# Distances in four row groups and messages by Strassen's product between the gates' products, in the last phase of a two-layer graph network

## The chip, the cores and the metric

The kernel runs on one core of a Trainium2 chip. The metric is the device time of one execution in microseconds (us), and less is better. A core has five engines, each with its own queue that it works through in order: PE (TensorE, matrix products; its weight loads are listed as PEld), DVE (VectorE), ACT (ScalarE), POOL (GpSimd) and SP (which here issues DMAs). They wait for each other by semaphores. PE writes only to PSUM, which has eight banks of 512 float32 values on each of 128 partitions; DVE and ACT read PSUM, POOL doesn't.

## The reference

There are 128 graphs of 128 nodes with 256 features, all in float32. Layer 0 mixes a graph product with a dense one under a gate, then a layer norm. Layer 1 is the part that matters here (the batch dimension is left out):

```python
s = x @ w_se.T + b_se                                   # 3 coordinates per node
sq = sum(s * s)
dist = sq[:, None] + sq[None, :] - 2.0 * s @ s.T
A = exp(-dist) * mask                                   # mask is the adjacency
msg = relu(x @ w_msg.T + b_msg)                         # 256 -> 256
x_nmp = A @ msg
x_conv = relu(bn(conv1d(relu(bn(conv1d(x, w1))), w2, 17 taps)) + x)
gi = concat(x_conv, x_nmp) @ w_ih.T + b_ih              # 512 -> 768
gh = x @ w_hh.T + b_hh                                  # 256 -> 768
r, z = sigmoid(gi_r + gh_r), sigmoid(gi_z + gh_z)
n = tanh(gi_n + r * gh_n)
x = layernorm(x + (1 - z) * n + z * x)
```

## The kernel before

Three phases follow one another. The first (to some 745 us) computes layer 0 and the first convolution, two graphs at a time, and stores x, its transpose and, in `H`, spectral coefficients. The second (L503 to L530) does the 17-tap convolution as products of coefficients. The third, from L601 on, is the one that is changed. It works on groups of G = 4 graphs, 32 groups (`g`), and the order of PE's work in it is written out by hand (`manual_schedule`, L830 to L859); the order on the other engines is left to the scheduler.

For a group g the loop does, on PE: `l1_gather(g)` (L748), which multiplies messages by the kernel matrix `AT`, 8 products of 128 columns; the messages of the next group, `l1_project(g+1)` (L693), 8 products of 256 columns into two banks; the first half of the gates, `l1_gru(g, 0)` (L775); the distances of the next group, `l1_kernel(g+1)` (L735), one product of 512 columns over all 128 rows; after every odd group the convolution's way back for two groups, `l1_synth` (L662); and the second half of the gates, `l1_gru(g, 1)`.

The gates use Strassen's product already: a 2x2 block product is made from seven products of sums of blocks. `l1_sums` (L762) makes four sums of each left factor (kind "h" of x1T and "c" of the convolution on POOL, "m" of the gathered messages on DVE), `l1_factors` (L617) those of the weights. `product(i)` (L781) then accumulates three products of 384 columns in one bank, and DVE combines the seven banks: L797 to L801, L804 and L805, with two sums on POOL (L802, L803). The order of issue is 0, 1, 5, 6, 4, 3, 2. After that come the gates' functions, the "tail" of a half group: ACT L808, DVE L815 and L816, ACT L817, DVE L819 to L822, the norm's statistics on DVE (L247, L248), a power on POOL (L152, L153), DVE L255, ACT L257 and the store (L825).

PSUM in this phase is two pools of four banks. `psC` (`bankc`, L611) serves everything but the convolution: each product takes a bank that is given back when its last reader is done, and PE has to wait for that. `acc` (L608) holds the four banks of `l1_synth`, which DVE reads at L686.

For the distances, `left` and `right` (L542 on) hold eight values per node and graph. `l1_own` (L715) transposes 16 graphs at a time (128 rows: 16 graphs x 8 values), and POOL makes `own` (L729): 128 x 512, where for each of the four graphs all rows but its own eight are masked to zero. So one product over 128 rows gives four graphs' distances, and ACT takes the exponential (L743), DVE multiplies by the adjacency (L744).

Of the kernel before, what the change touches and what calls it, by code (L numbers as in the profile page):

```python
# [14 lines left out]
P = 128  # L15
D = 256
NC = D // P
J = 2
# [2 lines left out]
CO = 3  # L21
KD = 8
GD = P // KD
PAD = TAPS // 2
L = P + PAD
M = L
# [7 lines left out]
def gnn_layers_kernel(ctx: ExitStack, tc: tile.TileContext, a: dict, out: bass.AP):  # L34
# [332 lines left out]
    def l1_front(p):  # L367
        s = st[p]
        h = s["h"] = wk.tile([P, J, D], F32, tag="h", name=f"h_{p}")
        for j in range(J):  # L370
            ph = bank(f"conv1_ps_{p}_{j}")
            for c in range(NC):
                nc.tensor.matmul(  # L373
                    ph[:, 0 : D + CO], lhsT=s["x1T"][:, c, nodes(j)], rhs=conv1_w[:, c, :],
                    start=(c == 0), stop=(c == NC - 1),
                )
            nc.vector.tensor_tensor(h[:, j, :], ph[:, 0:D], shift1, ALU.add)
            nc.scalar.activation(coords[:, p * J + j, :], ph[:, D : D + CO], AF.Copy)
        nc.scalar.activation(h, h, AF.Relu)

    def l1_store(p):
# [173 lines left out]
    nc.vector.tensor_add(left[:, :, CO + 1], left[:, :, CO + 1], coords[:, :, 2])  # L555
    nc.vector.tensor_copy(right[:, :, CO], left[:, :, CO + 1])

    mask_i = cw.tile([P, GD], I32, tag="mask_i", name="mask_i")
    nc.gpsimd.iota(mask_i, pattern=[[-KD, GD]], base=0, channel_multiplier=1)
    mask_f = cw.tile([P, GD], F32, tag="mask_f", name="mask_f")  # L560
    nc.vector.tensor_copy(mask_f, mask_i)
    mask = cw.tile([P, GD], F32, tag="mask", name="mask")
    nc.vector.tensor_scalar(mask, mask_f, 0.0, None, ALU.is_ge)
    nc.vector.scalar_tensor_tensor(mask, mask_f, float(KD - 1), mask, ALU.is_le, ALU.mult)
    w_msg = weights("w_msgT", D)
    b_msg = rows("L1_gnn_b_msg", 0, D, cw)


    def gate_weights(name, lo_n, lo_rz):
# [35 lines left out]
    ci = cpool("ci", 3)  # L605
    cy = cpool("cy", 4)
    ck = cpool("ck", 2)
    acc = cpool("acc", 4, space=PSUM)  # L608
    psc = cpool("psC", 4, space=PSUM)

    def bankc(name):  # L611
# [2 lines left out]
    cs = cpool("cs", 1)  # L614
    factors = {}

    def l1_factors():  # L617

        for kind, w in (("h", w_hh), ("c", w_ih[:, 0:NC]), ("m", w_ih[:, NC : 2 * NC])):
            t = cs.tile([P, 4, 3 * P], F32, tag=f"t{kind}", name=f"t_{kind}")  # L620
            b11, b12, b21, b22 = (w[:, c, h, :] for c in range(NC) for h in range(2))
            nc.vector.tensor_sub(t[:, 0, :], b12, b11)
            nc.vector.tensor_sub(t[:, 1, :], b22, t[:, 0, :])
            nc.vector.tensor_sub(t[:, 2, :], b22, b12)
            nc.vector.tensor_sub(t[:, 3, :], t[:, 1, :], b21)
            factors[kind] = (b11, b21, b22, t[:, 3, :], t[:, 0, :], t[:, 1, :], t[:, 2, :])

    def load_c(g):
        s = st[g] = {}
# [30 lines left out]


    def l1_synth(d):  # L662
        pcs = {}
        for e in range(2):
            s = st[2 * d + e]
            for c in range(NC):
                pc = pcs[e, c] = acc.tile([P, 512], F32, tag="acc", name=f"conv2_ps_{2 * d + e}_{c}")
                for q in range(G):
                    nc.tensor.matmul(  # L669
                        pc[:, nodes(q)], lhsT=sy[2 * d + e][0][:, q, c * P : (c + 1) * P], rhs=S,  # L670
                        start=(q == 0), stop=False, skip_group_check=True,
                    )
        for q in range(G):
            for e in range(2):
                for c in range(NC):
                    k = slice(32 * (NC * e + c), 32 * (NC * e + c) + ML)
                    nc.tensor.matmul(
                        pcs[e, c][:, nodes(q)], lhsT=sy[2 * d + e][1][k, q, :], rhs=SL[k, :],
                        start=False, stop=(q == G - 1), skip_group_check=True,
                    )  # L680
        for e in range(2):
            s = st[2 * d + e]
            s["xcT"] = ck.tile([P, NC, G * P], F32, tag="xcT", bufs=3, name=f"xcT_{2 * d + e}")
            for c in range(NC):
                dst = s["xcT"][:, c, :]
                nc.vector.scalar_tensor_tensor(  # L686
                    dst, pcs[e, c], scale2[:, c : c + 1], s["x1T"][:, c, :], ALU.mult, ALU.add
                )
                nc.scalar.activation(dst, dst, AF.Relu, bias=shift2[:, c : c + 1])
            l1_sums(2 * d + e, "c", s["xcT"], nc.gpsimd)  # L690


    def l1_project(g):  # L693
        s = st[g]
        x1T = s["x1T"]
        l1_sums(g, "h", x1T, nc.gpsimd)
        msg = ck.tile([P, G, D], F32, tag="msg", name=f"msg_{g}")
        for pr in range(G // 2):
            pm = bankc(f"msg_ps_{g}_{pr}")
            for j in range(2):  # L700
                q = 2 * pr + j
                for c in range(NC):
                    nc.tensor.matmul(  # L703
                        pm[:, j * D : (j + 1) * D], lhsT=x1T[:, c, nodes(q)], rhs=w_msg[:, c, :],
                        start=(c == 0), stop=(c == NC - 1),
                    )
            nc.vector.tensor_tensor(
                msg[:, 2 * pr : 2 * pr + 2, :], pm.rearrange("p (j e) -> p j e", j=2),
                b_msg.unsqueeze(1).to_broadcast([P, 2, D]), ALU.add,
            )  # L710
        nc.scalar.activation(msg, msg, AF.Relu)
        s["msg"] = msg


    def l1_own(g):  # L715
        if g % (GD // G) == 0:
            pt = bankc(f"turn_ps_{g}")
            for i, v in enumerate((left, right)):
                nc.tensor.transpose(
                    pt[:, nodes(i)], v[:, g * G : g * G + GD, :].rearrange("p q k -> p (q k)"), ident  # L720
                )
            turned = ck.tile([P, 2, P], F32, tag="turned", name=f"turned_{g}")
            nc.scalar.activation(turned.rearrange("p i n -> p (i n)"), pt[:, 0 : 2 * P], AF.Copy)
            st["turned"] = turned
        turned = st["turned"]

        own = ck.tile([P, G, P], F32, tag="own", name=f"own_{g}")
        lo = g * G % GD
        nc.gpsimd.tensor_tensor(  # L729
            own, turned[:, 1, :].unsqueeze(1).to_broadcast([P, G, P]),  # L730
            mask[:, lo : lo + G].unsqueeze(2).to_broadcast([P, G, P]), ALU.mult,
        )
        st[g].update(turned=turned, own=own)

    def l1_kernel(g):  # L735
        s = st[g]
        turned, own = s["turned"], s["own"]
        pd = bankc(f"dist_ps_{g}")
        nc.tensor.matmul(  # L739
            pd, lhsT=turned[:, 0, :], rhs=own.rearrange("p q n -> p (q n)"), start=True, stop=True  # L740
        )
        AT = ck.tile([P, G * P], F32, tag="AT", name=f"AT_{g}")
        nc.scalar.activation(AT, pd, AF.Exp, scale=-1.0)  # L743
        nc.vector.tensor_mul(AT, AT, s["adjT"].rearrange("p q n -> p (q n)"))  # L744
        s["AT"] = AT

# [15 lines left out]
    def l1_sums(g, kind, src, engine):  # L762

        v = src.rearrange("p c (r j n) -> p c r j n", r=G // 2, j=2)
        a11, a12, a21, a22 = (v[:, c, :, j, :] for j in range(2) for c in range(NC))
        t = ck.tile([P, 4, G // 2, P], F32, tag=f"s{kind}", name=f"s{kind}_{g}")
        s1, s2, s3, s4 = (t[:, i] for i in range(4))
        engine.tensor_tensor(s1, a21, a22, ALU.add)
        engine.tensor_tensor(s2, s1, a11, ALU.subtract)
# [2 lines left out]
        st[g][f"f{kind}"] = (a11, a12, s4, a22, s1, s2, s3)  # L772


    def l1_gru(g, pr):  # L775
        s = st[g]
        x1 = s["x1"]
        y = ck.tile([P, 2, D], F32, tag="y", name=f"y_{g}_{pr}")
        add, sub = ALU.add, ALU.subtract

        def product(i):  # L781
            pg = bankc(f"g_ps_{g}_{pr}_{i}")
            for k, (kind, lo) in enumerate((("h", 0), ("c", P), ("m", P))):
                nc.tensor.matmul(  # L784
                    pg[:, lo : lo + 3 * P], lhsT=s[f"f{kind}"][i][:, pr, :], rhs=factors[kind][i],
                    start=(k == 0), stop=(k == 2), skip_group_check=True,
                )
            return pg
# [38 lines left out]
            del st[g]  # L827

    ND = NG // 2
    with tc.manual_schedule(engines={mybir.EngineType.PE}):  # L830
        load_c(0)
        load_c(1)
        load_y(0)
        for g in range(2):
            load_x1(g)
            l1_own(g)
        for g in range(2):
            l1_project(g)
        for g in range(2):
            l1_kernel(g)  # L840
        l1_factors()
        l1_synth(0)
        for g in range(NG):
            d = g // 2
            if g + 2 < NG:
                load_c(g + 2)
                if g % 2 == 0:
                    load_y(d + 1)
                load_x1(g + 2)
            l1_gather(g)  # L850
            if 2 <= g + 1 < NG:
                l1_own(g + 1)
                l1_project(g + 1)
            l1_gru(g, 0)
            if 2 <= g + 1 < NG:
                l1_kernel(g + 1)
            if g % 2 == 1 and d + 1 < ND:
                l1_synth(d + 1)
            l1_gru(g, 1)  # L859
# [42 lines left out]
```

## Time and profile before

| what | us |
|---|---|
| runs (3): lowest, median, highest | 2086.69, 2088.59, 2091.08 |
| profiled execution, its time | 2086.79 |
| profiled execution, its span | 2085.0 |
| mean granted TensorE clock | 0.994 of full |
| last phase, from the first message product to the end | 929.5 to 2085.0 |
| PE busy from 1000 to 2000 us | 1000.0 |
| DVE busy from 1000 to 2000 us | 700.5 |
| POOL busy from 1000 to 2000 us | 402.4 |
| ACT busy from 1000 to 2000 us | 266.1 |

The span goes from the first to the last instruction of the profiled execution; 1.8 us of its time lie outside. An engine's busy time is what its instructions took; a bracket behind a line of a timeline tells how long the engine sat idle before it and what ended the wait. A matmul of the program in float32 stands as two passes in the trace. Matmuls overlap, so their costs are read from the start of one to the start of the next.

### The profile page before, as it was taken

How to read it: one execution, taken by the hardware profiler on the slowest of the kernel's cores; microseconds unless marked ns; L12 is line 12 of the kernel's file. 1: busy time of each engine (PE TensorE's matmuls, PEld its weight loads, DVE VectorE, ACT ScalarE, POOL GpSimd, SP SyncE). 2: the span in 40 equal slices, each digit the busy share in tenths (PEclk: the TensorE clock that was granted, in tenths of full speed). 3: DMA queues.
4: the chain of work that ended last, by engine and by line, in shares of the span. 5: the costliest groups of instructions: out<-in, count | busy, mean ns of one | idle time of the engine just before them, and what ended most of it. 6: DMA issues, size and time to landing. Idle time of an engine off the chain costs nothing.

```text
span 2085.0 us, 27437 instructions
## 1 busy us (share of the span) xinstructions
PE 2043.7 (98%) x9025; PEld 1401.6 (67%) x9025; DVE 1433.0 (69%) x2856; ACT 744.0 (36%) x1484; POOL 672.9 (32%) x889
## 2 busy tenths in 40 slices
PE   8999999999999979999999999999999999999997
PEld 5666666766667658886666666666666666666664
DVE  7777777776777744447776766676767767766766
ACT  3555555555555511112222222222222222222221
POOL 1111111111111135553343444343434434443432
PEclk9999999999999999999999999999999999999999
DMA  3444444344444469993222122212212221221100
GB/s 117 137 145 138 137 147 144 133 144 137 140 145 133 153 228 318 305 302 119 62 82 68 54 74 72 69 60 72 78 51 75 70 73 56 67 72 56 36 25 21
DMA packets 191789, 235.39 MB, mean 113 GB/s; under 512 B 16400, under 2 KB 136736, under 8 KB 191648
## 3 DMA queue, kind: packets, MB, share of 16 engines
q1 hardware_dynamic: 186160, 229.44, 33.5%
q10 hardware_dynamic: 5488, 4.21, 0.7%
q8 instruction: 72, 1.18, 0.2%
q14 instruction: 69, 0.57, 0.1%
HBM read 129.77 MB, written 103.81 MB: 112 GB/s over the span
## 4 chain that ended last, share of the span: by engine, by line
PE 95%; DVE 2%; DMA 2%; ACT 1%; issue 1%; POOL 0%; POOLq 0%; ACTq 0%; DVEq 0%; SPq 0%
PE g_ps L784 42%; PE f_ps L303 10%; PE msg_ps L703 5%; PE gate_ps L308 5%; PE conv_ps L373 5%; PE y_ps L510 5%; PE mix_ps L329 3%; PE coef_ps L391 3%; PE nmp_ps L754 3%; PE conv_ps L669 3%; PE z_ps L523 2%; PE w_ps L408 2%; PE x1T_ps L270 2%; PE wl_ps L411 1%; PE xT_ps L270 1%; PE dist_ps L739 1%
## 5 line engine op out<-in xcount | busy, mean ns | idle before, releaser
L303 PE MATMUL f_ps<-w,xT 128*128 128x512 f32 x512 | 244.1, 600 | 0.1
L808 ACT ACTIVATE o<-o 128x1024 f32<-128x1024 f32 x64 | 67.6, 1057 | 335.6 <-DVE o L805 335.6
L152 POOL TENSOR_SCALAR rstd_b<-mv_b 128x2 f32<-128x2 f32 x64 | 12.2, 191 | 501.6 <-DVE mv_b L248 501.6
L152 POOL TENSOR_SCALAR rstd_a<-mv_a 128x2 f32<-128x2 f32 x64 | 12.2, 191 | 463.9 <-DVE mv_a L248 447.9
L784 PE MATMUL g_ps<-t_c,sc 128*128 128x384 f32 x384 | 155.2, 486 | 0.0
L784 PE MATMUL g_ps<-t_m,sm 128*128 128x384 f32 x384 | 155.2, 486 | 0.0
L784 PE MATMUL g_ps<-t_h,sh 128*128 128x384 f32 x384 | 155.2, 486 | 0.0
L257 ACT ACTIVATE y<-y,nb_b,rstd_b 128x256 f32<-128x256 f32 x128 | 69.9, 593 | 218.6 <-DVE nb_b L255 218.6
L308 PEld LDWEIGHTS gate_ps<-w,xT 128*128 128x128 f32 x512 | 98.2, 192 | 69.2 <-issue 61.8
L510 PE MATMUL y_ps<-wb,H 128*128 128x256 f32 x544 | 128.9, 380 | 4.7 <-DMA wb<-w_d 2.1
L308 PE MATMUL gate_ps<-w,xT 128*128 128x256 f32 x512 | 132.2, 381 | 0.0
L802 POOL TENSOR_TENSOR u<-u,p 128x512 f32<-128x512 f32 x64 | 81.1, 1267 | 155.4 <-DVE p L801 155.4
L303 PEld LDWEIGHTS f_ps<-w,xT 128*128 128x128 f32 x512 | 88.6, 192 | 62.6 <-issue 62.2
L312 ACT ACTIVATE hom<-f_ps,norm 128x256 f32<-128x256 f32 x128 | 60.5, 473 | 187.0 <-PE f_ps L303 187.0
L518 POOL TENSOR_TENSOR ws<-wb 128x512 f32<-128x512 f32 x67 | 94.8, 1416 | 88.7 <-PE z_ps L523 60.3
L373 PE MATMUL conv_ps<-conv_w,x1T 128*128 128x259 f32 x512 | 122.6, 381 | 0.0
L510 PEld LDWEIGHTS y_ps<-wb,H 128*128 128x128 f32 x544 | 102.8, 190 | 20.5 <-issue 5.1
L703 PE MATMUL msg_ps<-w_msgT_w,cx1T 128*128 128x256 f32 x512 | 115.6, 379 | 0.0
L784 PEld LDWEIGHTS g_ps<-t_m,sm 128*128 128x128 f32 x384 | 73.0, 190 | 50.9
L784 PEld LDWEIGHTS g_ps<-t_c,sc 128*128 128x128 f32 x384 | 73.0, 190 | 50.9
L784 PEld LDWEIGHTS g_ps<-t_h,sh 128*128 128x128 f32 x384 | 72.9, 190 | 50.9 <-issue 1.2
L373 PEld LDWEIGHTS conv_ps<-conv_w,x1T 128*128 128x128 f32 x512 | 97.2, 190 | 14.4
(219 smaller groups left out, 4622.4 us busy)
## 6 DMA issues: line engine op xcount, KB each, us to landing
wb<-w_d SPq DMA_DIRECT2D x68, 512.0 KB
w_d<-w_o SPq DMA_DIRECT2D x256, 128.0 KB
y_d<-yb SPq DMA_DIRECT2D x68, 256.0 KB
x<-in_x SPq DMA_DIRECT2D x64, 256.0 KB
x_d<-x SPq DMA_DIRECT2D x64, 256.0 KB
x1T_d<-x1T SPq DMA_DIRECT2D x64, 256.0 KB
cx1T<-x1T_d SPq DMA_DIRECT2D x64, 256.0 KB
yt<-y_d SPq DMA_DIRECT2D x32, 512.0 KB
```

The costliest lines, as they stand in the source:

```text
L257: nc.scalar.activation(dst[:, q, :], src[:, q, :], AF.Identity, bias=nb[:, q : q + 1], scale=rstd[:, q : q + 1],)
L270: nc.tensor.transpose(t[:, (c * J + j) * P : (c * J + j + 1) * P], src[:, j, c * P : (c + 1) * P], ident,)
L303: nc.tensor.matmul(pf, lhsT=xT[:, c, nodes(j)], rhs=w0[:, c, 0 : 2 * D], start=(c == 0), stop=(c == NC - 1),)
L308: nc.tensor.matmul(pg[:, j * D : (j + 1) * D], lhsT=xT[:, c, nodes(j)], rhs=w0[:, c, 2 * D : 3 * D], start=(c == 0), stop=(c == NC - 1),)
L329: nc.tensor.matmul(pm[:, j * D : (j + 1) * D], lhsT=adjT_[:, j, :], rhs=hom[:, j, :], start=True, stop=True,)
L373: nc.tensor.matmul(ph[:, 0 : D + CO], lhsT=s["x1T"][:, c, nodes(j)], rhs=conv1_w[:, c, :], start=(c == 0), stop=(c == NC - 1),)
L510: nc.tensor.matmul(py[:, blk, :], lhsT=coefs(blk if k == 0 else 2 * k + 1 - blk, c), rhs=w[:, c, blk, :], start=(c == 0), stop=(c == NC - 1),)
L518: nc.gpsimd.tensor_tensor(ws, w[:, :, 0, :], w[:, :, 1, :], ALU.add)
L703: nc.tensor.matmul(pm[:, j * D : (j + 1) * D], lhsT=x1T[:, c, nodes(q)], rhs=w_msg[:, c, :], start=(c == 0), stop=(c == NC - 1),)
L784: nc.tensor.matmul(pg[:, lo : lo + 3 * P], lhsT=s[f"f{kind}"][i][:, pr, :], rhs=factors[kind][i], start=(k == 0), stop=(k == 2), skip_grou ...
L802: nc.gpsimd.tensor_tensor(u4, u2, p5, add)
L808: nc.scalar.activation(rz, rz, AF.Tanh, scale=0.5)
```

## The change

Distances: the 16 transposed graphs are put in another order (`coords` gets a slot that is worked out from the graph's number), so that the four graphs of a group lie in four different groups of 32 rows. `own` becomes 128 x 128, made by one masked multiplication on POOL, and the product becomes four of 32 rows and 128 columns, each into a bank of its own; they use the four banks of `acc`, now one tile, in turn with the synthesis. `l1_own` is called two groups ahead, and the distances come right after the gather.

Messages: seven products of sums (of 128 columns, for each of two pairs of graphs) in place of eight blocks, from the same sums of x1T that the gates use, which are now made two groups ahead and kept in three buffers. DVE combines seven pieces of 128 x 256, with two sums on POOL. The products are made in four portions, each with a bank of `psC`: 0 and 1, 5 and 6, 4 and 3, and 2. A portion is issued ahead of each of the first four gate products of `l1_gru(g, 0)`. The sums of kind "m" get one buffer in place of two.

```diff
+            b = p * J + j
+            slot = b // GD * GD + b % G * GR + b % GD // G
+            nc.scalar.activation(coords[:, slot, :], ph[:, D : D + CO], AF.Copy)
...
-    acc = cpool("acc", 4, space=PSUM)
+    acc = cpool("acc", 1, space=PSUM)
...
+        def products(*which):
+            pm = bankc(f"msg_ps_{g}_{which[0]}")
+            for k, i in enumerate(which):
+                for r in range(2):
+                    nc.tensor.matmul(
+                        pm[:, (2 * k + r) * P : (2 * k + r + 1) * P],
+                        lhsT=s["fh"][i][:, r, :], rhs=m_factors[i], start=True, stop=True,
+                    )
...
+        pa, pb = products(0, 1)
+        v.tensor_tensor(u1, pa, bias_m[:, 0].to_broadcast([P, 2, P]), add)
+        v.tensor_tensor(o[:, :, 0, 0, :], pb, u1, add)
+        yield
+        pa, pb = products(5, 6)
+        v.tensor_tensor(u2, pa, u1, add)
+        v.tensor_tensor(u3, pb, u2, add)
+        yield
+        pa, pb = products(4, 3)
+        v.tensor_tensor(p5, pa, bias_m[:, 1].to_broadcast([P, 2, P]), add)
+        v.tensor_tensor(o[:, :, 1, 0, :], u3, pb, sub)
+        nc.gpsimd.tensor_tensor(u4, u2, p5, add)
+        nc.gpsimd.tensor_tensor(o[:, :, 1, 1, :], u3, p5, add)
+        yield
+        (pa,) = products(2)
+        v.tensor_tensor(o[:, :, 0, 1, :], pa, u4, add)
         nc.scalar.activation(msg, msg, AF.Relu)
...
+        own = ck.tile([P, P], F32, tag="own", name=f"own_{g}")
+        nc.gpsimd.tensor_scalar(
+            own, turned[:, 1, :], mask[:, g % GR : g % GR + 1], None, ALU.mult
+        )
...
+        pd = acc.tile([P, G, 512], F32, tag="acc", name=f"dist_ps_{g}")
+        for q in range(G):
+            k = slice(q * P // G, (q + 1) * P // G)
+            nc.tensor.matmul(
+                pd[:, q, 0:P], lhsT=turned[k, 0, :], rhs=own[k, :], start=True, stop=True
+            )
...
-    def l1_gru(g, pr):
+    def l1_gru(g, pr, between=()):
...
         def product(i):
+            next(between, None)
...
+                l1_own(g + 2)
+                l1_sums(g + 2, "h", st[g + 2]["x1T"], nc.gpsimd)
             l1_gather(g)
             if 2 <= g + 1 < NG:
-                l1_own(g + 1)
-                l1_project(g + 1)
-            l1_gru(g, 0)
-            if 2 <= g + 1 < NG:
                 l1_kernel(g + 1)
+            l1_gru(g, 0, l1_project(g + 1) if 2 <= g + 1 < NG else ())
```

At the start of the phase, where there are no gates yet, the first two groups' portions are issued one after another, each group followed by its distances.

## Prediction

> **What bounds the kernel now.** First the busy shares of the page, then the same by stretch of the last phase: the stretch table's columns are the stretch, its length, and busy time (instructions) of PE, weight loads, DVE, ACT and POOL, then TensorE's granted clock, DMA share and GB/s.
>
> ```profile
> PE 2043.7 (98%) x9025; PEld 1401.6 (67%) x9025; DVE 1433.0 (69%) x2856; ACT 744.0 (36%) x1484; POOL 672.9 (32%) x889
> ```
>
> ```profile
> 1500.00:2000.00 500.00, 500.00 (x2109) 329.77 (x2108) 349.50 (x631) 133.13 (x201) 200.17 (x239) 1.00 0.19 61
> ```
>
> PE has no idle at all over 500 us of the phase that is changed, at full clock, so a shorter product list shortens the kernel as long as PE stays fed. But DVE stands at 70% (349.5 of 500): it reads every product out of PSUM and does the gates' arithmetic, and an engine at 70% on average is at 100% somewhere. So next comes the timeline, by engine, for one even-numbered group (start, length, then the work; x16 counts passes, a product in the program being two passes):
>
> ```profile
> 1509.99 1.95 PE L754 MATMUL nmp_ps<-AT,msg 128*128 128x128 f32 x16
> 1511.77 3.62 PE L703 MATMUL msg_ps<-w_msgT_w,cx1T 128*128 128x256 f32 x16
> 1515.23 0.81 PE L784 MATMUL g_ps<-w_hhT_w,cx1T 128*128 128x384 f32 x2
> ...
> 1528.78 1.02 PE L739 MATMUL dist_ps<-own,turned 128*128 128x512 f32 x2
> 1529.63 0.81 PE L784 MATMUL g_ps<-w_hhT_w,cx1T 128*128 128x384 f32 x2
> ```
>
> Lengths overlap, so prices are start to start: gather 16 passes of 128 columns 1.78 (0.111 a pass), messages 3.46, distances 0.85; seven gate products take 13.55 (1515.23 to 1528.78), 1.935 each. Call T the end of the gather (here 1511.77). DVE from T on:
>
> ```profile
> 1512.15 0.71 DVE L815 SCALAR_TENSOR_TENSOR o<-o 128x512 f32<-128x512 f32 x1 [1.20 <-ACT o L808]
> 1512.79 0.95 DVE L770 TENSOR_TENSOR sm<-nmpT 128x256 f32<-128x256 f32 x1
> 1513.66 1.21 DVE L816 SCALAR_TENSOR_TENSOR o<-o 128x512 f32<-128x512 f32 x1
> 1514.80 0.95 DVE L768 TENSOR_TENSOR sm<-nmpT 128x256 f32<-128x256 f32 x1
> 1515.67 0.68 DVE L707 TENSOR_TENSOR msg<-msg_ps,L_gnn_b_msg_b 128x512 f32<-128x512 f32 x1
> ...
> 1518.74 0.68 DVE L707 TENSOR_TENSOR msg<-msg_ps,L_gnn_b_msg_b 128x512 f32<-128x512 f32 x1
> 1519.34 0.67 DVE L822 TENSOR_TENSOR y<-o,cx 128x512 f32<-128x512 f32 x1
> 1519.94 0.68 DVE L797 TENSOR_TENSOR u<-g_ps,bias 128x512 f32<-128x512 f32 x1
> 1520.54 0.73 DVE L247 BATCH_NORM_STATS2 stats_b<-y 128x6 f32<-128x256 f32 x2
> 1521.20 0.16 DVE L248 BATCH_NORM_AGGREGATE mv_b<-stats_b 128x2 f32<-128x6 f32 x1
> 1521.28 0.65 DVE L798 TENSOR_TENSOR o<-g_ps,u 128x512 f32<-128x512 f32 x1
> ```
>
> The reader is to see that there is no idle bracket after the first line: from T+0.38 DVE works without a gap through the gates' tail of the previous half group (L815 to L822), and reads the first gate product (L797) only at T+8.17, 2.8 us after PE finished it. Today that is harmless: messages come first, and PE asks for that bank again only for its fifth gate product, at T+3.46+4x1.935 = T+11.2.
>
> **The change, part by part.** PE's list first. *Messages*: 8 products of 256 columns (3.46) become 14 of 128 columns, 28 passes x 0.111 = 3.11: 0.35 less. *Distances*: one product of 512 columns (0.85) becomes four of 32 rows. The trace has two such row-group stages:
>
> ```profile
> 706.63 1.14 PE L408 MATMUL w_ps<-wt,T 17*128 17x512 f32 x8
> 707.71 1.04 PE L411 MATMUL wl_ps<-wt,TL 128*32 128x512 f32 x2
> ```
>
> Eight passes of 512 columns took 1.08 where one after another at 0.425 would take 3.40, and two rounds of four 0.85; so rounds run four at a time, with 0.23 on top. (L677, 32 passes of 128 columns, gives the same: 1.10 = 8 x 0.107 + 0.24.) Four products are 8 passes: 2 x 0.107 + 0.23 = 0.45, so 0.40 less; bounds 0.28 (a quarter of L677) and 0.89 (no overlap at all, 0.04 more than now). The Trainium skill, TensorEngine Tiling (Array Packing), Key Properties, speaks against small tiled stages: a change of tiling mode drains TensorE. The 0.23 agrees with such a drain; without the rule's drain the stage would be 0.21 and the kernel, were PE the bound, some 7 us shorter by that page.
>
> If PE stayed fed, a group would lose 0.75. It will not. The gate products (G1 to G7) now have the message portions M1 to M4 between them: distances, M1, G1, M2, G2, M3, G3, M4, G4 to G7; all go through the same four banks of PSUM. In the built program M3 takes M1's bank, G3 takes G1's, M4 takes G2's, G4 M2's. A portion fills a bank in 0.89 us where a gate product fills it in 1.935, so the ring comes round sooner. PE, unhindered, wants M1's bank at T+0.45+0.89+1.935+0.89+1.935 = T+6.1 and G1's at T+7.0 (0.89 later); today it wants G1's at T+11.2.
>
> And DVE, in the order it now has: the same tail, then M1's first read, L822, M1's second read, both L247, one L248, then G1's read (L797). The first L707 of the listing is replaced by the distances' multiplication (L744, also 128x512). From rows: M1's first read starts where the second L707 stood, T+6.97; start to start 0.33 for 128x256 (L769 to L820 in the trace) and 0.60 for 128x512: L822 at 7.30, M1's second read 7.90 to 8.31, L247 twice 8.23 to 8.89, L248 to 8.97, G1's read 8.97 to 9.65. So M3 starts at 8.36, not 6.1, and G3 at 9.7, not 7.0. Then the second L248 and M2's first read, and L255, which must wait for POOL's two small operations: L255 starts 1.10 after L248 ends in the trace (its idle bracket), here at 10.84. Behind it in DVE's queue stands G2's read, 10.91 to 11.59, and M2's second, to 11.92. G3 ends at 11.63, M4 11.65 to 12.1, G4 to G7 4 x 1.935 = 7.74, to 19.85; two restarts at about 0.1 (the first pass after the 0.20 idle at 946.41 lasted 0.10 longer) make 20.0. Before, the half group with messages and distances ended at 3.46+13.55+0.85 = T+17.85. **An even group costs 2.15 more**, though PE has 0.75 less to do.
>
> Odd groups: the tail there is less slowed by POOL. Over 26 groups of the trace G1's read starts at T+8.17 in even groups, T+7.05 in odd ones, and T+8.65 in every second odd one, where POOL makes two 128x512 masks (L729, 1.04 each and more); these masks shrink to 128x128, so I take 7.05 for all odd groups: everything is 1.12 earlier, the group costs 2.15-1.12 = 1.03, say 1.05, more. 15 even and 15 odd groups carry messages between gates (groups 1 to 30): 15 x 2.15 + 15 x 1.05 = **+48**.
>
> The second half group has no portions; G1's bank is asked for 7.74 after its product starts, as now. With the synthesis (L669, L677) before it DVE is done 0.5 before PE asks (1503.65 against 1504.18): the distances no longer stand ahead of it (PE 0.85 sooner), nor L744 (DVE 0.6 sooner). Margin about 0.2: nothing added, at most 0.5 x 15 = 8.
>
> Edits with one answer: coordinates' slots, sums of x1T a group earlier (POOL at 40%, inputs landed a group ahead), one set of gathered sums instead of two (PE has read the old set before the gather ends), distances in the synthesis' four banks (13 us apart): nothing, hidden under PE. DVE gets 7 reads of 128x256 (0.41) for 2 of 128x512 (0.68), +1.5 a group, counted above where it stands ahead of a bank. POOL gets two sums of 0.73 and loses about as much on the masks.
>
> *Start of the phase*: no gates yet, so portions wait for DVE and POOL openly. POOL makes 12 sums (0.73 each, from 928.0) before the first mask, so first distances at 937.4; the second group's four portions (3.1), its distances, and the exponential that frees the banks put the synthesis at about 942.6, against 938.1: +4.5 (0 if POOL's order cost nothing, 8 if a load is late).
>
> Sum: span 2085.0 + 48 + 4.5 = 2137.5. The profiled execution took 2086.79, 1.8 over its span, and the median of the runs, 2088.59, another 1.8: 2137.5 + 3.6 = **2141**. The bounds of DVE's tail: at the unslowed lengths (0.42 for the L770 and L768 sums, 0.69 for L816) it ends 1.2 sooner, 36 us over 30 groups, but odd groups have little left to win: 15 x 1.2 + 15 x 0.5 = 26 less, 2115. With every odd group as at T+8.65, 15 x 1.6 = 24 more, 2165.
>
> **Rivals.** *DVE keeps up* (faster): it decides if M1 is read by T+6.1 and G1 by T+7.0. Then 30 x 0.75 = 22 less and 4.5 more at the start: 2071. For it: PE's list is surely shorter. Against: even the best row (7.05 + 0.8 + 0.68) frees G1 at 8.5. *The clock falls*: PE would idle 2.3 us in even groups, 1.1 in odd. The trace has an idle of 1.79 (at 774.15) after which four passes took 1.10 against 1.03, and one of 3.38 (at 17.25) after which PE lost some 1.8 in the next 4 us. 2.3 is nearer to the first, so I take nothing; else 15 x 1.8 = 27 more, 2168, and at most 30 x 1.8 = 54, 2195. The Trainium skill, TensorE: Matmul & The Clock Gate, Why this matters for your kernels, wants no idle above some 3 us; by that page also nothing is added. *Row groups do not overlap*: in groups that wait for DVE the distances lie before the wait, so 0.45 or 0.89 gives the same 2141; only if DVE kept up would it cost 30 x 0.44 = 13, 2084.
>
> **How the numbers follow.** Forecast 0.70 (own range 2115 to 2165); clock 0.12; DVE keeps up 0.10, with overlap or without; a wait so small that gain and loss cancel 0.03; a still shorter tail, 2095 to 2115, 0.05. Range 2105 to 2195. Some 0.2% is what a measurement of this kernel tells from no change: faster 0.10, within 0.03, slower 0.87.
>
> **What would show it.** In the changed profile PE's busy share in the last phase falls below 95%, with idle ended by DVE ahead of the third portion (released by its second message read) and of the third gate product (by L797's successor), near 2.3 and 0.4 us in even groups, less in odd; a group pair takes some 3.2 us longer. Distances start to start near 0.45, a portion 0.89. Wrong if PE shows no idle between portions, or if first reads of G1 start before T+7.

## The result, and the profile after

The changed kernel takes **2161.46 us** (median of 4 runs, 2159.23 to 2165.97) against 2088.74 us for the kernel before (4 runs, 2086.69 to 2091.08): a ratio of 1.0351, with a 95% interval of 1.033 to 1.0372. The span of the profiled execution is 2161.0 us, where it was 2085.0, and the mean granted TensorE clock 0.986, where it was 0.994.

The page of the changed kernel first: busy shares, and the shares of the chain of work that ended last.

```profile
PE 2060.4 (95%) x9601; PEld 1414.4 (65%) x9601; DVE 1476.9 (68%) x3024; ACT 745.0 (34%) x1484; POOL 722.4 (33%) x953
...
PE 68%; DVE 17%; POOL 5%; issue 3%; ACT 3%; DMA 3%; SPq 0%; ACTq 0%; POOLq 0%; DVEq 0%
```

The same stretch of the last phase as before, in the stretch table:

```profile
1500.00:2000.00 500.00, 474.95 (x2233) 313.92 (x2233) 345.92 (x661) 124.25 (x187) 205.48 (x246) 0.99 0.20 62
```

And the waits of PE from 940 to 2100 us (who waited for whom: us in total, times, longest):

```profile
PE msg_ps L717 <- DVE msg L730: 54.7, 30, 2.8
```

PE, which had no idle here, now idles 25 of 500 us, and the chain runs through DVE for 17% of the span. All of the named wait has one place, ahead of a message portion (L717), and one releaser, DVE's second read of a portion (L730). It comes once in each of the 30 groups that carry portions. The timeline of PE for an even-numbered group shows which portion:

```profile
1550.84 1.95 PE L790 MATMUL nmp_ps<-AT,msg 128*128 128x128 f32 x16
1552.72 0.50 PE L773 MATMUL dist_ps<-own,turned 32*128 32x128 f32 x8
1553.15 1.16 PE L717 MATMUL msg_ps<-w_msgT_w,cx1T 128*128 128x128 f32 x8
1554.15 0.81 PE L823 MATMUL g_ps<-w_hhT_w,cx1T 128*128 128x384 f32 x2
...
1556.09 1.05 PE L717 MATMUL msg_ps<-t_msg,sh 128*128 128x128 f32 x8
1556.98 0.81 PE L823 MATMUL g_ps<-w_hhT_w,cx1T 128*128 128x384 f32 x2
...
1558.27 0.81 PE L823 MATMUL g_ps<-w_ihT_w,nmpT 128*128 128x384 f32 x2
1561.87 1.20 PE L717 MATMUL msg_ps<-t_msg,sh 128*128 128x128 f32 x4 [2.79 <-DVE msg L730]
1562.86 1.06 PE L717 MATMUL msg_ps<-t_msg,cx1T 128*128 128x128 f32 x4
1563.71 1.48 PE L823 MATMUL g_ps<-t_h,sh 128*128 128x384 f32 x2
1564.99 0.85 PE L823 MATMUL g_ps<-t_c,sc 128*128 128x384 f32 x2
```

With T = 1552.72, the first and second portion and two gate products go through, and the third portion stands 2.79 us. Read on behind the idle: its two halves take 0.99 and 0.85 from start to start, 1.84 together, where the second portion took 0.89 for as much, and the first third of the gate product after them 1.28 where it takes 0.645. For some 3 us the products run at half speed. The stretch table shows why: the granted clock of this stretch is 0.50.

```profile
1561.65:1565.06 3.41, 3.19 (x11) 2.61 (x12) 2.60 (x10) 0.57 (x2) 0.92 (x2) 0.50 0.41 154
```

So the wait has a second price. This group has the longest idle of all; 13 of the even groups from 2 to 28 have 2.50 to 2.65, group 30 has 0.66. DVE in the same group:

```profile
1553.36 1.06 DVE L854 SCALAR_TENSOR_TENSOR o<-o 128x512 f32<-128x512 f32 x1 [1.20 <-ACT o L847]
...
1557.21 0.68 DVE L780 TENSOR_TENSOR AT<-AT,cadjT 128x512 f32<-128x512 f32 x1
...
1560.38 0.41 DVE L729 TENSOR_TENSOR mu<-msg_ps,L_gnn_b_msg_b 128x256 f32<-128x256 f32 x1
1560.72 0.67 DVE L861 TENSOR_TENSOR y<-o,cx 128x512 f32<-128x512 f32 x1
1561.32 0.41 DVE L730 TENSOR_TENSOR msg<-msg_ps,mu 128x256 f32<-128x256 f32 x1
...
1562.39 0.65 DVE L836 TENSOR_TENSOR u<-g_ps,bias 128x512 f32<-128x512 f32 x1
```

From the first line to the first gate product's read (L836) DVE has no idle. It works off the tail of the previous half group and the distances' multiplication (L780), and comes to the first portion, whose last pass on PE ends at 1554.31, only at 1560.38.

Where the 76.0 us of the span came from, measured from gather to gather:

| part | before | after | times | sum |
|---|---|---|---|---|
| even groups with portions, mean | 33.19 | 36.66 | 15 | +52.1 |
| odd groups with portions (with the synthesis), mean | 38.16 | 39.44 | 15 | +19.1 |
| first gather of the phase | 942.87 | 948.11 | 1 | +5.2 |
| group 0, whose gates carry no portions | 29.45 | 28.98 | 1 | -0.5 |

### The profile page after: what moved, and what is told of

Read it like the earlier page. It is cut to its first block, busy times and chain, and to the rows that moved or that the text cites. A ratio compares the mean times of both kernels' runs of the same rounds, so it can differ in the third digit from the quotient of the medians.

```text
span 2161.0 us, 28880 instructions
## 1 busy us (share of the span) xinstructions
PE 2060.4 (95%) x9601; PEld 1414.4 (65%) x9601; DVE 1476.9 (68%) x3024; ACT 745.0 (34%) x1484; POOL 722.4 (33%) x953
## 3 DMA queue, kind: packets, MB, share of 16 engines
q8 instruction: 77, 1.26, 0.2%
## 4 chain that ended last, share of the span: by engine, by line
PE 68%; DVE 17%; POOL 5%; issue 3%; ACT 3%; DMA 3%; SPq 0%; ACTq 0%; POOLq 0%; DVEq 0%
PE g_ps L823 27%; PE f_ps L304 10%; PE y_ps L513 5%; PE conv_ps L374 5%; PE gate_ps L309 5%; PE mix_ps L330 3%; PE coef_ps L394 3%; PE z_ps L526 2%; ACT o L847 2%; DVE o L855 2%; PE w_ps L411 2%; DVE o L854 2%; PE x1T_ps L271 2%; PE wl_ps L414 1%; DVE o L860 1%
## 5 line engine op out<-in xcount | busy, mean ns | idle before, releaser
L823 PE MATMUL g_ps<-t_h,sh 128*128 128x384 f32 x384 | 162.9, 507 | 2.4
L717 PE MATMUL msg_ps<-t_msg,sh 128*128 128x128 f32 x384 | 58.9, 293 | 57.4 <-DVE msg L730 54.7
L717 PEld LDWEIGHTS msg_ps<-t_msg,sh 128*128 128x128 f32 x384 | 53.1, 202 | 83.1 <-issue 71.0
```

What stands on the lines that cost most here:

```text
L717: nc.tensor.matmul(pm[:, (2 * k + r) * P : (2 * k + r + 1) * P], lhsT=s["fh"][i][:, r, :], rhs=m_factors[i], start=True, stop=True,)
L823: nc.tensor.matmul(pg[:, lo : lo + 3 * P], lhsT=s[f"f{kind}"][i][:, pr, :], rhs=factors[kind][i], start=(k == 0), stop=(k == 2), skip_grou ...
```

## The experiments

The theory: PE stands because portions and gate products share a ring of four PSUM banks that DVE empties behind the previous half group's tail, and most of the longer of these idles lower PE's clock. The rivals: DVE's load of seven message reads in place of two is itself too much; the new products are dear on PE by themselves; the distances' move is the loss. Each run's ratio is to the kernel before, run beside it on the same chip.

**1. One product later, same ring (shift1).** The portions stand ahead of the second to fifth gate product:

```diff
+    def later(n, portions):
+        for _ in range(n):
+            yield
+        yield from portions
...
-            l1_gru(g, 0, l1_project(g + 1) if 2 <= g + 1 < NG else ())
+            l1_gru(g, 0, later(1, l1_project(g + 1)) if 2 <= g + 1 < NG else ())
```

> Control for the run with banks of their own: the portions stand ahead of the second to fifth gate product as there, but still in the common ring of four banks. If it is the ring that counts, TensorE still waits in every group (the third portion and the product after it stand behind the bank of the first portion and of the second gate product, which VectorE empties behind the same tail): between 2120 and 2170 us. If it was only the order (one product later), it falls to about 2070 us like the run with banks of their own.

Measured: 2124.13 us (2 runs), ratio 1.0175 (1.0153 to 1.0198). The waits of PE in the last phase:

```profile
PE g_ps L823 <- DVE u L836: 32.7, 29, 2.0
```

The wait is still in nearly every group, now ahead of the third gate product and for the first gate product's reader (L836). So a shift alone gives back half of the loss, and the ring remains.

**2. Three products later, same ring (late).** As above with `later(3, ...)`: the portions stand ahead of the fourth to seventh gate product.

> The changed kernel with its portions ahead of the fourth to seventh gate product, in the common ring. By the theory TensorE asks for the first gate product's bank at about 7.2 us after the gather, and VectorE, with no message read in front of that read, frees it at about 8 us in even groups and 7 us in odd ones: a wait of under 1 us in even groups, hardly any in odd ones, so 2070 to 2100 us, far below the changed kernel. By the rivals (VectorE's load, or dear products) it stays near 2160 us.

Measured: 2090.14 us, ratio 1.0012 (1.0002 to 1.0022). DVE's reads and PE's products are as many as in the changed kernel, and all but 3 of its 73 us are gone. The waits of PE in the last phase:

```profile
PE g_ps L823 <- DVE u L836: 5.4, 14, 0.4
PE g_ps L823 <- DVE sm L805: 1.6, 7, 0.2
```

Even groups (33.6 and 33.75) wait a little and are 0.5 us longer than before; odd ones (37.5 and 37.72) don't wait and are 0.56 shorter. That a group without a wait is shorter speaks against dear products; that the time falls this far with the same reads, against DVE's load.

**3. Banks of their own (banks, then banks2).** From the third group on the portions go to the four `acc` banks, which hold the distances and the synthesis and are idle in between; one product later, as in run 1, which is the control for it. In the first form the four banks were one tile:

```diff
+            if g < 2:
+                pm = bankc(f"msg_ps_{g}_{which[0]}")
+            else:
+                if not own_banks:
+                    four = acc.tile([P, 4, 512], F32, tag="acc", name=f"msg_ps_{g}")
+                    own_banks.extend(four[:, n, :] for n in range(4))
+                pm = own_banks.pop(0)
```

> The changed kernel with one thing different: from the third group on the four message portions are written into the four PSUM banks that the distances and the synthesis use (idle while a half group's gates run), and stand ahead of the second to fifth gate product instead of the first to fourth. TensorE's products and VectorE's reads are the same in number and size. Theory (TensorE waits because portions and gate products share a ring of four banks that VectorE empties late): the idle ahead of the portions is gone, TensorE is near 99% busy in the last phase, and the kernel falls below the one before: 30 groups x 0.75 us less, 5 us more at the start of the phase, near 2070 us. Rival (VectorE's load of seven reads instead of two is itself too much): the wait only moves to another product, the time stays above 2130. Rival (the new products are dear on TensorE by themselves, by their row groups or their small size): also unchanged, near 2160, with TensorE busy and not idle.

Measured: 2246.89 us, ratio 1.0764 (1.0748 to 1.078), far from what any theory gave. The waits of PE:

```profile
PE msg_ps L725 <- DVE msg L738: 118.2, 30, 4.9
```

This is the *second* portion waiting for the reads of the *first*, although they lie in different banks: in the program the second portion's first product waits on VectorE's semaphore for the read of the first. The two are parts of one tile, and with four tiles, below, that wait is gone. The run prices a longer wait, and says nothing on the ring. The second form has four separate tiles:

```diff
-    acc = cpool("acc", 1, space=PSUM)
+    acc = cpool("acc", 4, space=PSUM)
...
+                pm = acc.tile([P, 512], F32, tag="acc", name=f"msg_ps_{g}_{which[0]}")
...
+        pd = [acc.tile([P, 512], F32, tag="acc", name=f"dist_ps_{g}_{q}") for q in range(G)]
...
+        for q in range(G):
+            nc.scalar.activation(AT[:, nodes(q)], pd[q][:, 0:P], AF.Exp, scale=-1.0)
```

> As the first run with banks of their own, but the four banks are four separate tiles (the distances too, with four exponentials of 128x128 instead of one of 128x512), since as parts of one tile the program made the second portion wait until VectorE had read the first. Theory: TensorE is fed, and only its own list counts: in the trace of the run with portions before the fourth to seventh gate product, groups without a wait are 0.57 us shorter than before (the distances bring 0.2 instead of 0.4), so 30 x 0.57 = 17 us less and 5 more at the start of the phase: near 2076 us. Rival (VectorE's seven reads are too much wherever the banks are): TensorE idles again ahead of a gate product, 2100 us or more.

Measured: 2075.33 us (5 runs, 2071.82 to 2077.1), ratio 0.994 (0.9927 to 0.9953). In the stretch table PE is busy without gap at full clock, and DVE busier than in either kernel (369.72 of 500):

```profile
1500.00:2000.00 500.00, 500.00 (x2408) 336.42 (x2407) 369.72 (x709) 139.55 (x249) 228.30 (x271) 1.00 0.20 61
```

With the ring parted and nothing taken from DVE or PE, the loss turns into a gain. Against run 1, which differs only in the banks and in the four tiles and four exponentials that go with them, it is 49 us. That shows the ring as the cause, and DVE's load falls as a rival. A pair of groups takes 70.14 to 70.35 us where it took 71.25 to 71.47, so 0.56 less a group.

**4. PE kept busy through the wait (fill).** In even groups from the third on, the second portion's products are issued four times with the same values: useless work of 2.67 us.

```diff
+            again = 4 if which[0] == 5 and g % 2 and g > 1 else 1
+            for k, i in [(k, i) for _ in range(again) for k, i in enumerate(which)]:
```

> The changed kernel, but in every even-numbered group from the third on the products of the second portion are issued four times (same values, 24 more passes of 128 columns, 2.67 us of work that adds nothing), so that TensorE is busy while the third portion's bank is still being read. If the time is set by the bank's release and TensorE's clock falls after the idle of 2.5 to 2.8 us (some 1.5 us lost in 10 of 15 even groups), the work is free and the fall goes: 10 to 15 us less than the changed kernel, near 2148 us. If the clock had no part in it, the time is the changed kernel's or up to 5 us more. If TensorE's own work bounded the kernel, 15 x 2.67 = 40 us more, near 2200 us.

Measured: 2152.17 us, ratio 1.0308 (1.0293 to 1.0323), where the changed kernel has 1.0351 (1.033 to 1.0372): 9 us *less* with more work. The timeline of PE in an even group:

```profile
1551.04 3.73 PE L718 MATMUL msg_ps<-t_msg,sh 128*128 128x128 f32 x32
...
1556.82 0.68 PE L718 MATMUL msg_ps<-t_msg,sh 128*128 128x128 f32 x4
1557.34 0.61 PE L718 MATMUL msg_ps<-t_msg,cx1T 128*128 128x128 f32 x4
```

The extra passes fill the idle, and the third portion's halves start 0.52 apart instead of 0.99. The 14 even groups from group 2 to 28 all take 35.73 to 36.01 us; in the changed kernel four of them take 35.76 to 35.89 and ten 36.85 to 37.57. The mean granted clock is 0.993 again (0.986). The trace's clock record has a stretch at half clock behind the idle in exactly these ten groups of the changed kernel, and in none of the groups here. So the slow products behind the idle were the clock, and it cost 14 x 1.05 = 15 us of the span, by the means of these groups (36.86 and 35.81).

**5. The first portion taken out of its bank by ScalarE (act).**

```diff
+            if g > 1 and which[0] == 0:
+                out = ck.tile([P, 512], F32, tag="mev", bufs=1, name=f"mev_{g}")
+                nc.scalar.activation(out, pm, AF.Copy)
+                pm = out
```

The adjacency tiles got two buffers in place of three to make room.

> The changed kernel, but ScalarE copies the first portion out of PSUM into a buffer of its own, from which VectorE reads it; so the bank of the first portion is free long before the third portion asks for it. Theory: there are two waits in a row, and with the first gone the third gate product still waits until VectorE has read the first gate product behind the same tail: the idle moves from the third portion to the third gate product, and the time falls by little, to 2130 to 2160 us. If only the third portion's wait counted, 30 groups lose their idle of 1.2 to 2.7 us, and it falls to about 2090 us.

Measured: 2169.44 us (2 runs), ratio 1.04 (1.0379 to 1.042), 8 us more than the changed kernel. The waits of PE in the last phase:

```profile
PE g_ps L827 <- DVE u L840: 65.2, 30, 3.1
```

The third portion goes through, and the idle stands one step on, ahead of the third gate product, as large as before. The two waits lie in series behind the same tail of DVE, as expected; that it grew (2.84 to 3.12 in the even groups from 2 to 28, from 2.50 to 2.79) was not.

**6. Each part alone (d_alone, m_alone).** The distances in row groups with the old messages, and the portions with the old distances.

```diff
             l1_gather(g)
             if 2 <= g + 1 < NG:
-                l1_own(g + 1)
+                l1_kernel(g + 1)
+            if 2 <= g + 1 < NG:
                 l1_project(g + 1)
             l1_gru(g, 0)
-            if 2 <= g + 1 < NG:
-                l1_kernel(g + 1)
```

> The kernel before with the distances alone changed: four products of 32 rows in separate row groups, in the synthesis' four banks, ahead of the messages; messages as eight products of 256 columns after the gather, as before. Theory (the new products are cheap, and TensorE stays fed): 32 groups x 0.40 us = 13 us less, some 2 us given back at the start, near 2077 us. Rival (row groups do not overlap): no change, near 2088 us. Rival (the change's loss comes with the distances' new place and their banks): above 2100 us.

Measured: 2090.44 us, ratio 1.0019 (1.0009 to 1.0028): no gain. The timeline of PE in an even group tells why:

```profile
1584.87 1.95 PE L766 MATMUL nmp_ps<-AT,msg 128*128 128x128 f32 x16
1586.75 0.50 PE L749 MATMUL dist_ps<-own,turned 32*128 32x128 f32 x8
1587.18 3.72 PE L713 MATMUL msg_ps<-w_msgT_w,cx1T 128*128 128x256 f32 x16
1590.74 0.81 PE L799 MATMUL g_ps<-w_hhT_w,cx1T 128*128 128x384 f32 x2
...
1593.96 0.81 PE L799 MATMUL g_ps<-w_ihT_w,nmpT 128*128 128x384 f32 x2
1594.86 0.91 PE L799 MATMUL g_ps<-t_h,sh 128*128 128x384 f32 x2
```

The distances' own step is 0.43, but the gather ahead of them takes 1.88 instead of 1.78 and the messages behind them 3.56 instead of 3.46. So they cost 0.63, and save 0.22 against 0.85. And the third gate product starts 0.90 after the line before it instead of 0.645, and itself takes 0.10 more: it waits for the first message bank, for which DVE, with the adjacency's multiplication now ahead, comes later. 0.22 saved, 0.36 lost. Odd groups keep the 0.22, and a pair of groups takes what it took before (71.27 to 71.37 us, but for two pairs). The first gather of the phase starts 20.1 us after the turn of the coordinates (13.7 before).

For the portions alone, the diff is the change's without the parts on distances (`own`, `turned` with one buffer each, and made a group ahead).

> The changed kernel with the old distances (one product of 512 columns after the half group's gates, in the common ring, masks of 128x512 on GpSimd) and the new messages in portions between the gate products. Theory (the portions in the common ring are the loss): slower than before, with TensorE idle ahead of the third portion or third gate product; VectorE has no distances' multiplication in front of the message reads, so the wait is somewhat shorter than in the changed kernel, but 0.40 us a group is lost again on the distances: 2130 to 2165 us. Rival (the distances' move is the loss): at or below the time before, 2077 to 2090 us.

Measured: 2124.79 us (2 runs), ratio 1.0186 (1.0165 to 1.0206). Even groups take 34.65 us (33.2), with 1.05 of idle ahead of the third portion; odd ones 38.62 (38.16); the first gather comes at 953.25, where the distances waited 5.4 us for GpSimd. So in the groups the portions alone lose 27 us, the distances alone nothing, and both together 71: the two are not additive. In the timelines of DVE the second read of the first portion ends in even groups at T+6.7 with the portions alone and at T+8.7 to T+9.0 in the changed kernel, where the adjacency's multiplication (L780) and more of the tail stand ahead of it.

**7. The old distances, PE fed (olddist).** Run banks2 with one product of 512 columns, in the same place:

```diff
-        for q in range(G):
-            k = slice(q * P // G, (q + 1) * P // G)
-            nc.tensor.matmul(
-                pd[q][:, 0:P], lhsT=turned[k, 0, :], rhs=own[k, :], start=True, stop=True
-            )
+        nc.tensor.matmul(
+            pd, lhsT=turned[:, 0, :], rhs=own.rearrange("p q n -> p (q n)"), start=True, stop=True
+        )
```

> As the first run of this call, but the distances are one product of 512 columns and 128 rows again, in the same place after the gather, with masks of 128x512 on GpSimd. It prices the row groups where TensorE is fed: by the prediction's 0.40 us a group it is 12 us slower than the run beside it, by the 0.22 us that the starts in the trace show (0.10 more on the gather's end and on the next product's beginning) 7 us slower, and equal if the row groups bring nothing.

Measured: 2088.95 us, ratio 1.0007 (0.9998 to 1.0015), 13.6 more than banks2. But the time alone misleads: a pair of groups takes 70.59 to 70.82 us, 0.46 more, so 0.23 a group and 7 us in all, which is the 0.22 of the starts. The other 7 lie at the start of the phase, where the first distances waited 5.5 us for the large mask.

**8. The start of the phase (best, then best2).** The first two groups' messages as eight products of 256 columns. First on top of banks, with its fault in the tile:

> The run with banks of their own for the portions, and the first two groups' messages as before (eight products of 256 columns, two reads): there are no gates yet beside which their portions could run. Theory: the 5 us at the start of the phase are given back in part: 2 to 4 us below the run with banks of their own, near 2067 us, below both kernels. If the start costs by the order of GpSimd's sums alone, the same as that run.

Measured: 2247.93 us, ratio 1.0777 (1.0761 to 1.0793); the start got no shorter (the distances stood behind GpSimd's sums). Then on top of banks2, with the first two groups' masked coordinates on VectorE:

```diff
+        (nc.vector if g < 2 else nc.gpsimd).tensor_scalar(
             own, turned[:, 1, :], mask[:, g % GR : g % GR + 1], None, ALU.mult
```

> As the run beside it, with the first two groups' messages as eight products of 256 columns and the first two groups' masked coordinates made by VectorE instead of GpSimd, so that the distances do not stand behind GpSimd's sums at the start of the phase. Theory: the 5 us at the start become about 1: near 2072 us, below both kernels. If the start is bound by something else (the synthesis' inputs), the same as the run beside it.

Measured: **2069.67 us** (5 runs, 2068.21 to 2072.7), ratio 0.9915 (0.9902 to 0.9929), below both kernels. From the turn of the coordinates to the first gather it is 14.3 us (18.4 in banks2, 13.7 before).

## Why the prediction was right, and where its sum was short

The mechanism was right: portions and gate products go round the ring faster than DVE, and PE stands ahead of the third portion (runs 1, 2 and 3 show it). The time, 20 us above the forecast, lies in the range. What came is the forecast's wait together with the clock's fall, to which as a rival I gave a chance of 0.12. Step by step:

- **A portion at 0.89**: 0.89 (1556.09 to 1556.98). Right.
- **Distances at 0.45, so 0.40 less**: mis-sized. The stage itself took 0.43, but the products on both sides of it took 0.10 more each: 0.63, so 0.22 less (runs 6 and 7). The 0.23 that I put on top, read from stages of the earlier phase, held the stage's own overhead and not its neighbours'. It was hidden here, since PE waited anyway. With PE fed a group gains 0.56, not 0.75, so the rival "DVE keeps up" would have been 2075 (run banks2), not 2071.
- **Even groups, DVE frees the first portion's bank at T+8.3 and PE wants it at T+6.1**: PE wants it at T+6.2. The third portion started at T+8.86 to T+9.01 in 13 of the even groups from 2 to 28, and at T+9.15 in the one shown, 0.5 to 0.8 later than the sum made it (8.36). In the 13 DVE's tail started no later than before (T+0.07 or T+0.29, against T+0.38). What was mis-sized is the multiplication by the adjacency. I gave it the 0.60 from start to start of the message read whose place it took; there it took 1.13 (1.21 long, where that read was 0.68):

```profile
1250.89 1.21 DVE L780 TENSOR_TENSOR AT<-AT,cadjT 128x512 f32<-128x512 f32 x1
```

The group shown above is the exception: L780 took 0.68 in it, but the tail started at T+0.64 and its first operation took 1.06 (0.71). Even groups at full clock cost some 2.6 more, not 2.15: 14 x 0.47 = 7 us. Group 30 cost only 0.7 more. The wait of 0.4 ahead of the third gate product is there too, 0.25 and 0.10 for the restart in groups at full clock.
- **The clock, taken as nothing**: this is the step of the sum that failed. I set the idle of 2.3 us beside the one of 1.79 that had cost nothing and not beside the one of 3.38 that had cost 1.8. It came to 1.05 a group in run 4's comparison: 15 of the 23.5 us by which the span (2161.0) is over the sum (2137.5). The trace of the kernel before held a third idle, which I passed over. It is shorter than both (1.57, ended at 494.16), and from 1.15 us after its end on the granted clock was 0.50:

```profile
494.16 0.33 PE L270 MATMUL x1T_ps<-ident,x 128*128 128x128 f32 x1 [1.57 <-ACT x L257]
495.31:498.72 3.41, 3.41 (x6) 1.45 (x5) 2.34 (x4) 0.22 (x1) 0.30 (x1) 0.50 0.40 129
```

The rival's own price (27 us by 1.8 each, 2168) was nearer to the truth than the forecast. The Trainium skill, TensorE: Matmul & The Clock Gate, Why this matters for your kernels, asks for no idle above some 3 us. These idles were 2.5 to 2.8, and ten of 14 lowered the clock, so the measurement decides against using the rule as a threshold. The same page, A second HAM failure mode: psum-queue depth-cycling, tells of a bf16 kernel that cycles through PSUM banks, in which frequent short idles between groups of products let the clock go up and down. This float32 kernel is like it: the idles come at a ring of banks, once in a group.
- **Odd groups at +1.05**: +1.28, with an idle of 1.14 to 1.26. Near.
- **Start of the phase at +4.5**: +5.2. Near. With the first two groups' messages as before and their masked coordinates off GpSimd, most of it went (best2 in run 8); with the messages alone it did not (best).
- **The synthesis, nothing added**: inside the groups no wait is named there. Right.

What stays open: why the multiplication by the adjacency takes 1.21 us in those 13 even groups and 0.68 in odd ones (in even groups POOL's sums run beside it, but no run shows that they are the reason), and why the tail of group 16, the one shown, starts later than the others'.

## What to carry to other kernels

When short products are put between long ones, follow the ring of PSUM banks and not the sum of the work: count how soon PE comes back to a bank, and set it against the place of that bank's reader in the reader's own queue. An engine at 70% can hold an engine at 100% for microseconds when its oldest work stands in front; here a pool of their own for the short products turned +3.5% into -0.6% with nothing else saved. And price an idle of the matrix engine twice, once for its length and once for the slower clock behind it.

## What was not expected of the hardware

- **The clock falls after idles well under 3 us, and not each time.** Counted by the length of the group behind the idle, among the 14 even groups from 2 to 28: none after 1.03 to 1.05 us (portions alone), 3 after 1.75 to 2.02 (shift1), 10 after 2.50 to 2.79 (the changed kernel), and all after 2.84 to 3.12 (act). Behind such an idle a product of 384 columns took 1.28 instead of 0.645, for some 3 us.
- **It counts where an idle falls in time, and not its length alone.** In the changed kernel idles of 2.50 and of 2.63 us both lowered the clock and didn't. By the trace's clock record the stretches at half clock in its groups 1 to 30 last 3.41 us each, and they start whole multiples of 3.413 us apart (1486.56 and 1561.65: 22 times that). Lay that grid over the 14 idles, and each is cut in two. In the ten that lowered the clock the longer piece is 1.62 to 2.57 us, in the four others 1.47 to 1.57. In shift1 the border lies higher: of four pieces of 1.88 to 1.91 three lowered the clock, and pieces up to 1.76 didn't. So these figures are no threshold for other kernels.
- **A stage of row groups costs its neighbours.** 0.10 on the last product before it and 0.10 on the first after it, on top of its own 0.43.
- **A mask of a quarter the size was no cheaper on GpSimd.** The 128x128 multiplication by a value per row (L762) took 1.36 us in the mean of 32, the 128x512 one by a spread mask (L729 before) 1.20.
